# Dense chunks of a two-layer transformer kernel keep their GpSimd form through the MoE routing, and the chunks are shared out anew over the stages

## The chip, the core and the metric

The kernel runs on one core of a Trainium2 chip. A core has a matrix engine (TensorE, in the profile PE, its weight loads PEld), VectorE (DVE), ScalarE (ACT), GpSimd (POOL) and SyncE (SP), which only issues transfers here. Every engine works through its own queue in order, and engines wait for each other through semaphores. The metric is the device time of one execution in microseconds; less is better.

## What is computed

The input is x with 4 sequences of 512 tokens and 256 features, all in float32. Two layers are added to it:

```python
xn = layernorm(x)
x = x + linear_attention(xn) + top32_gene_ffn(xn)          # layer 0
xn = layernorm(x)
x = x + attn_with_dense_ffn(xn) + moe(xn)                  # layer 1
# attn_with_dense_ffn: q,k,v; y = sigmoid(q) * cumsum(exp(k) v) / cumsum(exp(k))
#                      x + (u * silu(g)) @ w_out.T,  u,g = split(y @ w_swiglu.T)
# moe: 16 experts, the best 2 for each token, and one shared expert of twice the width
```

The part that matters here is layer 1. Each token goes through a dense feed-forward (1024 hidden features) and the shared expert (352 hidden features). It also goes through two of 16 experts, for which the tokens are first sorted by expert.

## The kernel before, in words

**Dense chunks.** The dense feed-forward and the shared expert of layer 1 are worked off together by the generator `dense()`. A half is 256 tokens; there are 8 halves, and each has 11 chunks of up to 128 hidden features, 88 chunks in all, numbered here from 0. For one chunk, `up` makes gate and up products in a PSUM bank pair `gu` (matmuls at L583, three such buffers), then tanh at L587 (tile `th`, two buffers), then the hidden tile `hid` (four buffers). `down` (L606), which runs two chunks behind, adds the chunk's contribution to the PSUM accumulator `acc`. After a half's eleventh chunk, L617 adds `acc` to x.

**Two forms of a chunk.** From `gu` and `th` to `hid` there are two ways. In the DVE form (L590, L591) VectorE reads `gu` straight from PSUM in two operations, and `gu` is free when these are done. In the POOL form ScalarE copies `gu` to SBUF (L594, tile `both`), which frees `gu`, and GpSimd does three operations (L595 to L597). The list `calm` says which: as long as it is empty, chunks take the POOL form; L705 fills it.

**Order.** The stages are written as generators and woven together by `together`; `d(n)` gives the next n chunks to a stage. This source order is a priority: when the program is built, the language's scheduler sets the order on each engine, and it moves chunks forward to where it reckons an engine to be free. The chunks are given out so: 40 in the mixing of both layers (L644 to L702), 5 beside the routing (L706), 15 beside the scatters (L708), 6 behind them (L710), and 22 behind the experts.

**Mixing, routing, scatters, experts.** `mix(3, 0, NT)` is the last mixing stage. Its end is on VectorE: scans at L426, reciprocals at L435 and products at L433 and L437, which make `yT`. `route` then counts tokens for each expert: two matmuls on PE (L491, L492) with matrices that GpSimd makes (L472 to L488), a copy of the counts (L494), and a row of small VectorE operations to `slot` (L538), the row of the sorted list to which each token goes. `scatter` writes the tokens there with 32 indirect transfers from GpSimd's queue (L549). These are paced: each also waits for the latest `down` that the source order had reached (`beat`). When all have landed, `fetch` (L741, SyncE's queue) reads the sorted tokens two tiles at a time. The experts run from the transpose at L733 through L770 to L791 and L802. Behind them come the last 22 chunks, beside the gathers of the results (L836).

**Memory.** `const` and `wd` are pools that live to the end; `wk` and `w2` belong to the mixing and are closed at L703, and the pool of the routing takes their place. The constant tile `ones` is read by the scans of the first layer (L274) and of the mixing (L426).

## Time and profile before

| what | value |
|---|---|
| median of 5 runs (lowest, highest) | 589.59 us (588.74 to 589.77) |
| the profiled execution's own time | 589.25 us |
| its span in the profile | 587.5 us |
| mean granted TensorE clock | 0.985 of full speed |
| busy: PE, DVE, ACT, POOL | 540.1, 342.3, 265.8, 235.9 us |
| 88 chunks: up matmuls, L583 | 124.3 + 49.6 us |
| 88 chunks: down matmuls, L606, most of them | 68.5 us |
| POOL form, L595, 40 chunks | 29.7 us, 742 ns each |
| DVE form, L590, 48 chunks | 20.0 us, 418 ns each |
| scatters, L549 | 32 of 966 ns |

PE is busy for 92% of the span, so what is left of the time lies mostly in places where PE stands idle or its clock is halved. The busy share of a span counts matmuls whose ends are modelled. A wait that a view puts down to an engine is put down to the last releaser that the profile knows.

### The profile page before, as it was taken

To read this page: it belongs to the slowest core of one execution; us is meant where nothing else is said; L and a number is where in the kernel's file an instruction comes from. 1 tells how busy PE (TensorE), PEld (TensorE's weight loads), DVE (VectorE), ACT (ScalarE), POOL (GpSimd) and SP (SyncE) were. 2 spreads that over 40 slices of the span, in tenths; PEclk is the share of its full clock that TensorE was granted. 3 is DMA by queue.
4 is the path that set the end of the run, shared out by engine and by line. 5 is a ranking of instruction groups with operands and counts; after the bars stand their busy time and mean duration, and the time that the engine had idled before them with its cause. 6 is when DMAs were issued, how large, how long until landed. Compare 5 with 4: busy or idle time off the path is not lost.

```text
span 587.5 us, 7343 instructions
## 1 busy us (share of the span) xinstructions
PE 540.1 (92%) x2360; PEld 387.7 (66%) x2360; DVE 342.3 (58%) x890; ACT 265.8 (45%) x568; POOL 235.9 (40%) x298
## 2 busy tenths in 40 slices
PE   3958979899999998999899859999999999999997
PEld 1424447655676565766676648887777777788886
DVE  3899998379691948963681786332222222226563
ACT  3667864865447582477348401113333333321111
POOL 1333049476747345573784115770000000007561
PEclk9998979999999999999999979999999999999999
DMA  5993000000000000000029701224333333113541
GB/s 165 388 382 119 1 1 1 1 1 1 1 1 1 0 2 1 2 0 1 0 61 324 206 1 64 103 104 125 90 108 108 108 108 99 55 64 109 142 134 45
DMA packets 38453, 47.38 MB, mean 81 GB/s; under 512 B 4016, under 2 KB 34960, under 8 KB 38160
## 3 DMA queue, kind: packets, MB, share of 16 engines
q1 hardware_dynamic: 35344, 38.53, 20.2%
q0 software_dynamic: 3072, 8.39, 4.7%
q8 instruction: 19, 0.31, 0.2%
q14 instruction: 18, 0.15, 0.1%
HBM read 28.30 MB, written 18.61 MB: 80 GB/s over the span
## 4 chain that ended last, share of the span: by engine, by line
PE 50%; DVE 27%; POOL 7%; ACT 7%; issue 4%; DMA 3%; SPq 0%; POOLq 0%; DVEq 0%; ACTq 0%
PE gu L583 12%; PE pu L770 9%; PE py L791 7%; PE acc L606 6%; PE pm L389 5%; DVE rep L312 5%; DVE top L311 5%; PE pt L733 4%; POOL ys L836 3%; DVE sums L435 3%; DVE sums L426 2%; PE pm L224 2%; PE pm L334 1%; DVE bs L203 1%; DMA wqkv<-in_wqkv_dram 1%
## 5 line engine op out<-in xcount | busy, mean ns | idle before, releaser
L583 PE MATMUL gu<-yT,wugt 128*128 128x256 f32 x512 | 124.3, 381 | 0.0
L583 PEld LDWEIGHTS gu<-yT,wugt 128*128 128x128 f32 x512 | 95.6, 190 | 13.6 <-issue 1.4
L587 ACT ACTIVATE th<-gu 128x256 f32<-128x256 f32 (+1 forms) x88 | 33.7, 383 | 150.8 <-PE gu L583 124.9
L836 POOL DMA_INDIRECT ys<-yrows,slot x32 | 30.3, 948 | 147.1 <-PE acc L606 142.8
L606 PE MATMUL acc<-wot,hid 128*128 128x256 f32 x256 | 68.5, 385 | 8.0 <-DVE hid L591 8.0
L770 PE MATMUL pu<-wex,xgT 128*128 x188 | 63.8, 461 | 0.8 <-ACT xgT L747 0.8
L606 PEld LDWEIGHTS acc<-wot,hid 128*128 128x128 f32 x256 | 47.8, 192 | 15.6 <-DVE hid L591 8.4
L583 PE MATMUL gu<-xn1T,sgu 128*128 128x256 f32 (+1 forms) x192 | 49.6, 394 | 0.1
L779 DVE TENSOR_TENSOR hb<-pu,hb 128x176 f32<-128x176 f32 x47 | 16.0, 341 | 51.0 <-ACT hb L778 51.0
L389 PE MATMUL pm<-w,xn1T 128*128 128x512 f32 (+1 forms) x128 | 44.1, 494 | 0.5 <-ACT xn1T L377 0.5
L791 PE MATMUL py<-wex,hgT 128*128 x188 | 44.5, 379 | 0.0
L595 POOL TENSOR_TENSOR hid<-both 128x256 f32<-128x256 f32 (+1 forms) x40 | 29.7, 742 | 33.5 <-ACT both L594 33.3
L590 DVE SCALAR_TENSOR_TENSOR th<-th,gu 128x256 f32<-128x256 f32 (+1 forms) x48 | 20.0, 418 | 39.2 <-ACT th L587 38.9
L583 PEld LDWEIGHTS gu<-xn1T,sgu 128*128 128x128 f32 (+1 forms) x192 | 35.5, 190 | 9.1 <-issue 2.6
L791 PEld LDWEIGHTS py<-wex,hgT 128*128 128x128 f32 x188 | 35.7, 190 | 8.6 <-issue 0.2
L770 PEld LDWEIGHTS pu<-wex,xgT 128*128 128x128 f32 x188 | 32.0, 190 | 11.0 <-ACT xgT L747 1.0
L549 POOL DMA_INDIRECT xrows<-xn,slot x32 | 30.9, 966 | 20.4 <-DVE th L590 10.9
L389 PEld LDWEIGHTS pm<-w,xn1T 128*128 128x128 f32 x128 | 24.0, 190 | 21.6 <-issue 16.5
L783 DVE COPY hgT<-pt 128x512 f32<-128x512 f32 (+1 forms) x24 | 16.3, 680 | 34.3 <-PE pt L733 34.3
L283 PE MATMUL pm<-wct,xnT 128*128 128x512 f32 x64 | 32.2, 637 | 1.2 <-ACT xnT L242 1.2
L311 DVE MAX8 top<-rep 128x8 f32<-128x512 f32 x48 | 32.6, 680 | 0.3
L312 DVE MATCH_REPLACE8 rep<-top,rep 128x512 f32<-128x512 f32 x48 | 32.3, 673 | 0.0
(170 smaller groups left out, 966.7 us busy)
## 6 DMA issues: line engine op xcount, KB each, us to landing
xrows<-zero SPq DMA_DIRECT2D x1, 6016.0 KB, 22.5
xg<-xrows SPq DMA_DIRECT2D x23, 256.0 KB, 2.8
yrows<-yg SPq DMA_DIRECT2D x23, 256.0 KB, 2.1
wex<-in_w_gate_up_dram SPq DMA_DIRECT2D x8, 704.0 KB, 10.6
xs<-in_x_dram SPq DMA_DIRECT2D x4, 512.0 KB, 7.7
wugt<-in_wug_dram SPq DMA_DIRECT2D x1, 2048.0 KB, 12.5
wex<-in_w_down_dram SPq DMA_DIRECT2D x4, 512.0 KB, 11.6
out_dram<-xs SPq DMA_DIRECT2D x7, 256.0 KB, 2.8
```

The lines of the kernel that those rows point to most:

```text
L283: T.matmul(pl, xnT[:, h, i * P : (i + 1) * P], wct[:, h], start=(h == 0), stop=(h == NH - 1))
L311: V.max(tp[:, 8 * r : 8 * r + 8], src)
L312: V.match_replace(rep, tp[:, 8 * r : 8 * r + 8], src, TAKEN)
L389: T.matmul(o[:, 0:n], xnT[:, h, i * P : (i + 1) * P], w1[:, h, at : at + n], start=(h == 0), stop=(h == NH - 1),)
L549: sc = G.indirect_dma_start(out=xrows, out_offset=bass.IndirectOffsetOnAxis(ap=slot[:, k, i : i + 1], axis=0), in_=xn1[:, i // NT, i % NT] ...
L583: T.matmul(gu[0:m, k], w[:, h, at : at + m], ins[which][:, h], start=(h == 0), stop=(h == NH - 1))
L587: S.activation(th[0:m], gu[0:m, 0], AF.Tanh, scale=0.5)
L595: G.tensor_tensor(hid[0:m], both[0:m, 0], both[0:m, 1], ALU.mult)
L606: mm = T.matmul(acc[:, t], hid[0:m, t * P : (t + 1) * P], dw[0:m, dc], start=(n == 0 and t == 0), stop=(n == NC - 1), skip_group_check=True,)
L770: T.matmul(pg[:, 0 : 2 * NI], xT[:, i, h], wex[:, bass.ds(at[i] + h * 2 * NI, 2 * NI)], start=(h == 0), stop=(h == NH - 1),)
L791: mm = T.matmul(py[:, i * D : (i + 1) * D], hT[:, i, h], wex[:, bass.ds(at[i] + EW - (2 - h) * D, D)], start=(h == 0), stop=(h == 1),)
L836: G.indirect_dma_start(out=ys[:, asked], out_offset=None, in_=yrows, in_offset=bass.IndirectOffsetOnAxis(ap=slot[:, k, n : n + 1], axis=0) ...
```

## The change

```diff
-    ones = const.tile([P, L], F32, name="ones")
-    G.memset(ones, 1.0)
...
+    ones = wk.tile([P, L], F32, name="ones")
+    G.memset(ones, 1.0)
...
-                both = w2.tile([P, 2, HB], F32, name="both")
+                both = wd.tile([P, 2, HB], F32, name="both")
...
-    together((m2, 9), (back(3, 0, NT), 12), d(9))
+    together((m2, 9), (back(3, 0, NT), 12), d(8))
...
-    together((m3, 9), d(5), (load_experts(), 17))
+    together((m3, 9), d(4), (load_experts(), 17))
     mixing.close()
     routing = ctx.enter_context(ExitStack())
-    calm.append(True)
     together((route(), 8), d(5))
     routing.close()
-    together((scatter(), 33), d(15))
-
-    run_all(islice(dd, 6))
+    calm.append(True)
+    together((scatter(), 33), d(18))
+
+    run_all(islice(dd, 5))
```

The five chunks that the source gives to the routing now take the POOL form, since `calm` is filled after the routing. Two chunks fewer are given to the mixing (38 in place of 40), so 43 chunks in all have the POOL form instead of 40. The scatters get 18 chunks in place of 15, and 5 in place of 6 follow them. The sum up to the experts stays 66. For the POOL form to work after the mixing's pools are closed, `both` moves to the pool `wd` (two buffers of 2 KB a partition), and to make room `ones` (2 KB) moves from `const` to `wk`, so that GpSimd fills it a little later. Nothing of the computation changes.

## The prediction

> **What bounds the kernel now.** I read the waits of PE first, because PE is busy for 92% of the span: its largest single wait behind the start is one of 8.0 us.

> ```profile
> PE acc L606 <- DVE hid L591: 8.0, 1, 8.0
> ```

> (engine, line, releaser; total, times, longest, in us.) The timeline shows where it lies: between the end of the last mixing and the routing.

> ```profile
> 334.33 1.89 PE L583 MATMUL gu<-yT,wugt 128*128 128x256 f32 x8
> 338.50 3.36 DVE L435 RECIPROCAL sums<-sums 128x256 f32<-128x256 f32 x2
> 341.77 1.16 DVE L426 TENSOR_TENSOR_SCAN sums<-ones,pm 128x512 f32<-128x512 f32 x1
> 342.85 0.40 DVE L590 SCALAR_TENSOR_TENSOR th<-th,gu 128x256 f32<-128x256 f32 x1
> 343.16 0.69 DVE L437 TENSOR_TENSOR yT<-sums 128x512 f32<-128x512 f32 x1
> 343.76 0.42 DVE L591 TENSOR_TENSOR hid<-gu,th 128x256 f32<-128x256 f32 x1
> 344.24 0.80 PE L606 MATMUL acc<-wot,hid 128*128 128x256 f32 x1 [8.02 <-DVE hid L591]
> ```

> (start, duration.) PE has made the up products of chunk 43 and then needs `hid` of chunk 41. That chunk has the DVE form, and its two operations stand behind the mixing's reciprocals and scan in VectorE's queue. Until they come, all three `gu` buffers are held and PE stands still. The table of stretches adds what follows (length, then busy PE, PEld, DVE, ACT, POOL, clock, DMA share, GB/s):

> ```profile
> 336.00:340.00 4.00, 0.22 (x1) 0.00 (x0) 4.00 (x4) 0.00 (x0) 0.00 (x0) 1.00 0.01 2
> 340.00:344.00 4.00, 0.00 (x0) 0.00 (x0) 4.00 (x6) 0.00 (x0) 0.00 (x1) 0.65 0.00 0
> 344.00:345.00 1.00, 0.76 (x2) 0.67 (x3) 0.82 (x3) 0.38 (x1) 1.00 (x5) 0.50 0.00 0
> 347.00:348.00 1.00, 1.00 (x4) 0.82 (x3) 0.62 (x2) 0.00 (x0) 0.00 (x0) 0.50 0.00 0
> 348.00:349.00 1.00, 1.00 (x6) 0.89 (x5) 0.93 (x3) 0.00 (x0) 0.00 (x0) 0.97 0.00 0
> ```

> The granted clock is halved from about 341.2 to 348.0, so PE also works slowly just when the routing needs it. ACT and POOL are idle here. From the routing on, two chains run to the experts: PE's chunks (2.59 us each: an up row at 361.39, the next at 363.98), and scatter and fetch:

> ```profile
> 347.27 0.42 DVE L494 COPY cnt<-pr 128x256 f32<-128x256 f32 x1 [1.49 <-PE pr L492]
> 356.24 0.17 DVE L538 TENSOR_SCALAR slot<-two 128x32 int32<-128x32 f32 x1
> 396.69 0.96 POOL L549 DMA_INDIRECT xrows<-xn,slot  x1 [0.30 <-issue]
> 399.24 0.88 SPq L741 DMA_DIRECT2D xg<-xrows  x2
> 405.26 0.27 PE L733 MATMUL pt<-ident,xg 128*128 128x128 f32 x1
> ```

> The first fetch is issued at 399.24 and lands 2.7 us later (the transfers of `xg`), at 401.94. PE takes it up at 405.26 without a wait. So today PE's chain ends last, and the scatter chain has only 3.3 us to spare. That number decides this case.

> **The change, part by part.** I read the order of the built program on each engine, before and after. Up to the last mixing's end (ACT's exponentials near 329.5) no engine's order or wait changes, apart from the start. The two chunks taken from the mixing in the source are therefore not taken from it in the program; what differs follows.

> *Three more POOL-form chunks, 40 to 42.* In PE's order, behind the up products of chunk 43, there now stand down 41, up 44, down 42 and up 45, and only then the down that waits for VectorE, now that of chunk 43. Are they fed? ACT copies `both` of chunk 40 after its exponentials (to 330.1), then tanh and copy of 41 (0.38 + 0.58 us, to 331.1), and of 42 once PE has made it (333.66, to 334.7). POOL ends L417 at 330.0 and needs 3 x 0.73 plus gaps, 2.35 us a chunk: `hid` 40 at 332.5, 41 at 334.9, 42 at 337.4. PE wants them at 333.46, 336.1 and 338.7. All are in time, with 0.9 us or more to spare. So PE works on to 334.33 + 3 x 1.73 + 2 x 0.86 = 341.2, and waits about 3.0 us in place of 8.0. VectorE's order behind it is the same, so `hid` (now of 43) still comes at 344.2. Gain for PE: two chunks, 5.2 us. The DVE operations of chunk 40, which go, stood at 326.42 and 326.88 in front of an idle stretch of 2.85 us: worth nothing.

> *The clock.* From PE's rows I listed the stretches of over 2.5 us in which PE runs nothing but transposes or nothing at all. After 221.07 to 224.04 (2.97 us) and 284.33 to 287.01 (2.68) the clock stays at 1.00. After 40.27 to 45.37 (5.10), 73.38 to 80.85 (7.47, with transposes in it) and 336.22 to 344.24 (8.02) it is halved, for 3.4 us once and 6.8 twice. The stretch here becomes 3.0 us, so the nearest row, 2.97, says that the clock stays. The bounds are that the drop stays (nothing gained) or goes. If it goes, L491 and L492, which lie on the way to `cnt`, take 0.43 us each as the full-speed rows of this shape (0.86 for four passes at L606) in place of 0.85 and 0.87, and the half `down` before them shrinks likewise. L491 must still wait for POOL's matrix (L472 to L473, ready at 344.6). I get `cnt` at 346.15 in place of 347.27: 1.1 us earlier. I take this value.

> [...]

> *The routing on VectorE.* From `cnt` to the end of `slot` the trace has 347.27 to 356.41, 9.14 us, with two pairs of chunk operations and L617 inside. After, L617 stands earlier but still inside, and there are two pairs and one more L590: 0.33 us more. `slot` ends at 346.15 + 9.14 + 0.33 = 355.6, against 356.41: 0.8 us earlier; 0.3 us later without the clock's gain.

> *Scatters.* POOL's interval is 1.265 us (395.43, 396.69). The pacing asks for 1.41 us each now (18 chunks of 2.59 for 33 steps), but it starts from earlier beats: the last scatter waits for down 57 in both programs, which was done near 389.9 before (six chunks before 405.42) and is two chunks earlier now. It waits for none. From the end of `slot` to the landing of the first `xg` is 401.94 - 356.41 = 45.5 us as before: landing at 401.1.

> *PE to the experts.* Behind 344.24 PE needs 0.43 each for half a down, L491, L492 and the other half, with the wait for POOL's matrix to 346.3, then 20 chunks of 2.59: 398.1. It therefore waits 3.0 us for `xg`, and the first transpose is at 401.2 against 405.26: **4.1 us earlier**. Of the 7.2 us that PE gains, the scatter chain lets 4.1 through.

> *Costs at nothing.* `ones` is filled after `zero` (0.30 us later); its first reader is at 24.9 us. The expert loads wait for other beats; they are issued to 323.8 and needed at 406. `both` in `wd` keeps two buffers. The fetches behind the first land at 402.7, 404.4 and 405.0 in the trace, 0.8 us earlier after; PE needs the second 2.6 us after the first, so they are in time. The experts and the last 22 chunks keep their order. Bounds for all of these together, from the runs' spread: 0.5 us either way.

> **Sum.** 589.25 - 4.1 = 585.15 for the profiled execution; the median lies 0.34 above that execution, so I forecast **585.5 us** (0.7% faster).

> **Rivals.**
> 1. *The clock takes part of it back* (0.24). If it drops at 341 all the same, `slot` ends at 356.74 and the transpose comes at 402.3: 3.0 us gained, 586.6. Or it drops ahead of the experts: there PE has nothing but transposes from 398.1 to the first L770 at 402.55 (1.35 us behind the first transpose, as 405.26 to 406.61), 4.45 us, which lies between the 2.97 that passed and the 5.10 that did not. Half speed for 3.4 to 6.8 us, less some stalls there, costs 1.5 to 3 us: 587.0 to 588.5. I give the forecast more, since 4.45 us is a drop in some executions at most and the median goes with the majority.
> 2. *PE sets the start of the experts* (0.04): 7.2 us, 582.4. It needs the scatters 3 us faster; at 0.96 + 0.30 us each nothing in the change does that.
> 3. *The chunks don't fill the hole* (0.09): ACT or POOL come late, PE waits for POOL where it waited for DVE, and the time stays at 589.6. Against: the margins above.
> 4. *Slower* (0.09): POOL's nine operations of 0.73 us, new between 330 and 337.4, hold up VectorE's scans and reciprocals, which are the path to `slot`. If each holds VectorE for its whole length, that is 6.6 us: `slot` at 363.3, `xg` at 408.9, 3.6 us later than 405.26: 593.2. It decides from 3.3 us on (`slot` behind 359.7). Against it stands a row pair:

> ```profile
> 227.23 3.33 DVE L435 RECIPROCAL sums<-sums 128x256 f32<-128x256 f32 x2
> 227.61 0.74 POOL L341 TENSOR_TENSOR xw<-xn,nwb 128x256 f32<-128x256 f32 x1
> ```

> With POOL beside it the pair of reciprocals takes 3.33 us, alone 3.36. Only L437 shows a longest of 1.41 us against a median of 0.68: 0.73 us is the most from one meeting, and POOL should be done at 337.4, before 337.9.

> [...]

> **How the numbers follow.** The forecast case has 0.54, between 584.4 and 586.3. The rivals have 0.24, 0.04, 0.09 and 0.09. The range 583.8 to 588.4 takes in the forecast and nearly all of rival 1 (0.77), and reaches a little towards 2 and 3. Faster by over 0.2% (1.2 us, about what a measurement of this kernel can tell): 0.54 + 0.24 + 0.04 = 0.82; same 0.09; slower 0.09.

> **What would show it.** PE's wait for `hid` L591 falls to about 3 us; the clock stays at 1.00 from 341 to 348; L595 runs 43 times; `slot` ends near 355.6; the first L733 is near 401.2, and PE or its weight load waits some 3 us there for the transfer of `xg`; everything behind is the same, 4.1 us earlier. The prediction is wrong if `slot` is later than in the trace of before, if the clock drops, or if PE doesn't wait for `xg`.

## The result, and the profile after

The changed kernel takes a median of 589.29 us (586.73 to 590.12, 24 runs). The kernel before, run beside it, takes 589.49 us (588.11 to 590.64, 44 runs). The ratio is 0.9994, with a 95% interval of 0.9988 to 1.0000: no difference by the bound of 0.2%. The profiled execution took 589.88 us, its span is 588.2 us. L595 runs 43 times.

The waits of PE after the change (engine, line, releaser; total, times, longest):

```profile
PE acc L606 <- DVE hid L591: 2.8, 1, 2.8
...
PE pt L733 <- DMA xg<-xrows: 2.7, 1, 2.7
```

The first part of the prediction came true to within 0.3 us: the wait for `hid` went from 8.0 to 2.8 us (predicted 3.0), and a new wait for the sorted tokens of 2.7 us (predicted 3.0) stands at L733. So PE's hole is filled as meant, and yet the time is the same. The timeline shows how far the gain gets:

```profile
344.82 0.99 PE L606 MATMUL acc<-wot,hid 128*128 128x256 f32 x2 [2.84 <-DVE hid L591]
...
347.55 0.42 DVE L494 COPY cnt<-pr 128x256 f32<-128x256 f32 x1 [1.20 <-PE pr L492]
...
357.14 0.17 DVE L538 TENSOR_SCALAR slot<-two 128x32 int32<-128x32 f32 x1
...
397.60 0.96 POOL L549 DMA_INDIRECT xrows<-xn,slot  x1 [0.30 <-issue]
...
402.97 0.97 PE L733 MATMUL pt<-ident,xg 128*128 128x128 f32 x4 [2.67 <-DMA xg<-xrows]
...
404.67 2.71 PE L770 MATMUL pu<-wex,xgT 128*128 x4 [0.73 <-DMA xg<-xrows]
```

The reader must look at the durations as well as at the starts. The four transposes at L733 take 0.97 us together and the four passes at L770 2.71 us. Before, the first four transposes took 0.60 us and the first four passes stood so:

```profile
406.61 1.45 PE L770 MATMUL pu<-wex,xgT 128*128 x4 [0.75 <-ACT xgT L747]
```

The table of stretches after the change says why (length, then busy PE, PEld, DVE, ACT, POOL, clock, DMA share, GB/s):

```profile
340.00:344.00 4.00, 1.98 (x10) 1.39 (x8) 4.00 (x5) 0.00 (x0) 0.00 (x0) 1.00 0.01 2
344.00:345.00 1.00, 0.18 (x1) 0.19 (x2) 1.00 (x3) 0.15 (x1) 0.45 (x3) 1.00 0.00 0
345.00:346.00 1.00, 1.00 (x3) 0.76 (x3) 0.82 (x4) 0.24 (x1) 1.00 (x3) 0.54 0.00 0
...
400.00:402.00 2.00, 0.30 (x2) 0.00 (x0) 0.74 (x2) 0.00 (x0) 0.00 (x0) 1.00 0.33 92
402.00:404.00 2.00, 0.97 (x4) 0.60 (x4) 0.00 (x0) 0.00 (x0) 0.00 (x0) 0.78 0.95 304
...
406.00:408.00 2.00, 2.00 (x7) 1.38 (x6) 0.23 (x1) 0.32 (x1) 0.00 (x0) 0.50 0.13 45
```

There are two drops of the granted clock. The first comes at 345.08, a quarter of a microsecond after PE has gone back to work, and lasts 3.4 us. Before, it lay at 341.24 to 348.07, so it has moved and become shorter, but it still lies on the two count matmuls ahead of `cnt`. The second is new: 403.11 to 409.94, 6.8 us, at the very start of the experts. There the kernel before had 1.00.

To compare milestones, each trace is shifted so that the start of its last operation at L352 (an addition on VectorE) falls on that of before (300.60). For this kernel that takes off 0.56 us; 0.32 us of it are there at the first matmul (10.06 against 9.74). Milestones below are in this common frame; times of drops and of profile lines are each trace's own. The last column is the 32nd matmul at L791, some 27 us into the experts.

| kernel | `cnt` L494 | `slot` ends | last scatter | first L733 | first L770 | 32nd L791 |
|---|---|---|---|---|---|---|
| before | 347.27 | 356.41 | 396.69 | 405.26 | 406.61 | 429.88 |
| after | 346.99 | 356.75 | 397.04 | 402.41 | 404.11 | 429.88 |

The experts start 2.85 us earlier (405.26 - 402.41), and at the 32nd matmul at L791 nothing is left of it. **The gain is made, and given back within the next 27 us.**

### The profile page after: what moved, and what is told of

Same layout as the page of the kernel before. It is cut to its first block, busy times and chain, and to the rows that moved or that the text cites. A ratio compares the mean times of both kernels' runs of the same rounds, so it can differ in the third digit from the quotient of the medians.

```text
span 588.2 us, 7352 instructions
## 1 busy us (share of the span) xinstructions
PE 543.7 (92%) x2360; PEld 389.6 (66%) x2360; DVE 340.3 (58%) x884; ACT 267.5 (45%) x571; POOL 242.4 (41%) x307
## 4 chain that ended last, share of the span: by engine, by line
PE 46%; DVE 24%; POOL 9%; DMA 8%; ACT 7%; issue 5%; SPq 1%; POOLq 0%; DVEq 0%
PE pu L770 10%; PE gu L583 8%; PE py L791 7%; PE pm L389 5%; DVE rep L312 5%; DVE top L311 4%; PE acc L606 4%; DMA xrows<-xn,slot 4%; PE pt L733 4%; DVE sums L435 3%; POOL ys L836 3%; DVE sums L426 2%; POOL xrows L549 2%; PE pm L283 2%; PE pm L224 2%
## 5 line engine op out<-in xcount | busy, mean ns | idle before, releaser
L583 PE MATMUL gu<-yT,wugt 128*128 128x256 f32 x512 | 124.2, 381 | 0.0
L583 PEld LDWEIGHTS gu<-yT,wugt 128*128 128x128 f32 x512 | 95.6, 190 | 13.6 <-issue 1.2
L606 PE MATMUL acc<-wot,hid 128*128 128x256 f32 x256 | 68.2, 384 | 2.9 <-DVE hid L591 2.8
L770 PE MATMUL pu<-wex,xgT 128*128 x188 | 65.9, 473 | 0.7 <-DMA xg<-xrows 0.7
L606 PEld LDWEIGHTS acc<-wot,hid 128*128 128x128 f32 x256 | 47.6, 191 | 10.4 <-DVE hid L591 3.2
L583 PE MATMUL gu<-xn1T,sgu 128*128 128x256 f32 (+1 forms) x192 | 49.5, 394 | 0.1
L595 POOL TENSOR_TENSOR hid<-both 128x256 f32<-128x256 f32 (+1 forms) x43 | 31.9, 742 | 33.6 <-ACT both L594 33.3
L791 PE MATMUL py<-wex,hgT 128*128 x188 | 44.5, 379 | 0.0
L583 PEld LDWEIGHTS gu<-xn1T,sgu 128*128 128x128 f32 (+1 forms) x192 | 35.4, 189 | 9.2 <-issue 2.6
L791 PEld LDWEIGHTS py<-wex,hgT 128*128 128x128 f32 x188 | 35.7, 190 | 8.6 <-issue 0.2
L770 PEld LDWEIGHTS pu<-wex,xgT 128*128 128x128 f32 x188 | 33.0, 196 | 11.4 <-ACT xgT L747 1.1
L549 POOL DMA_INDIRECT xrows<-xn,slot x32 | 30.9, 967 | 20.7 <-PE gu L583 12.5
L590 DVE SCALAR_TENSOR_TENSOR th<-th,gu 128x256 f32<-128x256 f32 (+1 forms) x45 | 18.7, 417 | 33.6 <-ACT th L587 33.6
L597 POOL TENSOR_TENSOR hid<-hid,th 128x256 f32<-128x256 f32 (+1 forms) x43 | 33.1, 770 | 3.2
L596 POOL TENSOR_TENSOR th<-th,hid 128x256 f32<-128x256 f32 (+1 forms) x43 | 32.4, 752 | 3.3
```

Source lines behind the costliest of these rows:

```text
L549: sc = G.indirect_dma_start(out=xrows, out_offset=bass.IndirectOffsetOnAxis(ap=slot[:, k, i : i + 1], axis=0), in_=xn1[:, i // NT, i % NT] ...
L583: T.matmul(gu[0:m, k], w[:, h, at : at + m], ins[which][:, h], start=(h == 0), stop=(h == NH - 1))
L595: G.tensor_tensor(hid[0:m], both[0:m, 0], both[0:m, 1], ALU.mult)
L596: G.tensor_tensor(th[0:m], th[0:m], hid[0:m], ALU.mult)
L597: G.tensor_tensor(hid[0:m], hid[0:m], th[0:m], ALU.add)
L606: mm = T.matmul(acc[:, t], hid[0:m, t * P : (t + 1) * P], dw[0:m, dc], start=(n == 0 and t == 0), stop=(n == NC - 1), skip_group_check=True,)
```

## The experiments

**The theory** from these profiles: filling the idle stretch works, but (a) the 2.84 us that are left of it still halve the clock ahead of `cnt`, so that the experts start 2.85 us earlier and not 4.1; and (b) the new wait of 2.67 us for `xg` halves the clock again, for 6.8 us at the start of the experts, which costs the 2.85 us. **The rivals:** the 2.85 us go to something else in the experts (fetches, other engines, the memory), whatever the clock does; or the new division of the chunks has a price of its own. Kernels that ran on the same chip are compared with the kernel before on that chip.

### The changed kernel again

No edit; it is the yardstick for the three that follow, on the same chip.

> The changed kernel as it is, beside the others on the same chip. Theory: 588 to 590 where the kernel before has 589.5; in its trace the clock drops behind PE's wait for xg and PE's gain of nearly 3 us at the first transpose is gone some 8 us later. If this chip holds the engines up beside the scatters as in the runs before (four idle stretches that no wait explains, 10 us in all), this control shows by how much.

Measured: 589.40 us against 589.80, ratio 0.9990 (0.9979 to 1.0000). In its profile the first drop begins at 343.76 and still stands from 348 to 349 (0.50), so it lasts over 5.2 us, `slot` ends at 358.04 and the first L733 is at 403.73, 1.5 us earlier than before; the second drop lasts 3.4 us (405.20 to 408.61), and the 32nd L791 is at 430.08, 0.2 us later than before. The two drops vary in length, and the gain is gone in this execution too: the longer first drop took more of it ahead of the experts, the shorter second one less behind (1.7 us).

### Work in place of the wait for the sorted tokens

The gate products of one chunk ahead of the experts are made three times more, into the same place with the same result, about 2.6 us of matmuls that nobody needs:

```diff
+    AGAIN = {65: 3}
...
-            for k, (w, at) in enumerate(((gw, g0), (uw, u0))):
+            pairs_ = ((0, gw, g0), (1, uw, u0))
+            for k, w, at in pairs_[:1] * again + pairs_:
...
-                behind.append((half, n, up(ins, bool(calm), *c)))
+                behind.append((half, n, up(ins, bool(calm), AGAIN.get(half * NC + n, 0), *c)))
```

(`up` gets the argument `again`; lines behind L583 are two further down in this kernel.)

> As e1: the changed kernel with 6 more matmuls in chunk 65, the last before the experts, so that PE isn't idle while it waits for xg. Theory: the clock stays at 1.00 from 400 to 410 and the time is 2.8 us below that of the changed kernel on the same chip. Rival: no difference, or slower by the added matmuls.

Measured: 586.97 us against 589.80, ratio 0.9953 (0.9939 to 0.9967): 2.8 us faster than the kernel before. Against the changed kernel on this chip (589.40) it is 2.4 us, by useless work alone; 2.8 were expected. Its timeline and stretches at the start of the experts:

```profile
404.02 1.44 PE L772 MATMUL pu<-wex,xgT 128*128 x4 [0.74 <-DMA xg<-xrows]
```

```profile
404.00:406.00 2.00, 1.98 (x9) 1.45 (x10) 0.16 (x1) 1.64 (x3) 0.00 (x0) 1.00 0.76 235
406.00:408.00 2.00, 1.98 (x8) 1.10 (x7) 0.53 (x2) 0.83 (x2) 0.00 (x0) 1.00 0.56 139
```

The four passes take 1.44 us instead of 2.71, and the clock stays at 1.00. In the common frame `slot` ends at 356.85 and the first L733 is at 402.45, as in the changed kernel to 0.1 us, while the 32nd L791 is at 427.08, which is 2.80 us earlier. The fetches were not changed, and the transfers' share in these two stretches is higher than in the changed kernel (0.76 and 0.56 against 0.63 and 0.13). So the second drop costs the 2.85 us, and the rival that puts them down to fetches or memory falls.

### A real chunk in place of the wait

```diff
-    run_all(islice(dd, 5))
+    run_all(islice(dd, 6))
```

> As e3: the changed kernel with 6 in place of 5 chunks behind the scatters, 21 in the tail. Theory: 5.4 us below the changed kernel on the same chip (2.8 for the clock, 2.6 for the chunk); rival (the clock costs nothing): 2.6 us below.

Measured: 583.47 us, ratio 0.9898 (0.9880 to 0.9916), 5.9 us below the changed kernel, where 5.4 were expected. The stretch 404 to 406:

```profile
404.00:406.00 2.00, 2.00 (x11) 1.42 (x10) 0.34 (x1) 1.64 (x3) 0.00 (x0) 1.00 0.49 149
```

The clock holds here too, and the 32nd L791 is 2.56 us earlier than before. A chunk that is done there is also missing at the end of the program, which by a chunk's length is worth another 2.59 us (an estimate). The rest of the 6.0 us by which this kernel is below the one before, about 1 us, lies behind the experts and was not followed.

### Both ends filled

The POOL form stays as in the changed kernel, but the mixing gets its 40 chunks back (45 of POOL form in all), the scatters 15, and 8 chunks follow them; the gathers at the end are paced for the two chunks fewer that are left there (two more lines, not shown).

```diff
-    together((m2, 9), (back(3, 0, NT), 12), d(8))
+    together((m2, 9), (back(3, 0, NT), 12), d(9))
...
-    together((m3, 9), d(4), (load_experts(), 17))
+    together((m3, 9), d(5), (load_experts(), 17))
...
-    together((scatter(), 33), d(18))
+    together((scatter(), 33), d(15))
...
-    run_all(islice(dd, 5))
+    run_all(islice(dd, 8))
```

> The changed kernel's forms and memory with the old split, so that 45 chunks have the POOL form and a third chunk stands in the stretch where PE waited, and with 8 chunks behind the scatters (68 before the experts, 20 in the tail, whose gathers and adds are paced a little faster to fit). Theory: PE has no idle stretch over 1 us at 342 nor ahead of the experts, the clock stays up at both, slot comes 1.5 us earlier than in the changed kernel, and the first transpose is near 401.3 where the kernel before has 405.3; with a tail two chunks shorter the time is 9 us below the kernel before: 580. Rival (the tail is then bound by the gathers, 32 at 1.27 us and what follows): 3 to 4 us of that are not won.

Measured: 579.60 us (579.39 to 580.07), ratio 0.9831 (0.9816 to 0.9847): 1.7% faster than both kernels, the fastest version here. Stretches and timeline:

```profile
345.00:346.00 1.00, 1.00 (x7) 0.87 (x6) 0.80 (x3) 0.00 (x0) 1.00 (x2) 1.00 0.00 0
...
402.00:404.00 2.00, 1.92 (x9) 1.45 (x10) 0.08 (x1) 1.63 (x3) 0.00 (x0) 1.00 0.64 161
```

```profile
400.75 0.60 PE L733 MATMUL pt<-ident,xg 128*128 128x128 f32 x4
```

PE has no wait for `hid` and none at the first L733, and the clock is 1.00 in both places. In the common frame `cnt` comes at 345.74 (1.53 us earlier than before), the first L733 at 400.80 (4.46 earlier) and the 32nd L791 at 425.40 (4.48 earlier): what is gained ahead of the experts now arrives behind them. With two chunks less at the end (2 x 2.59) that makes 9.7 us; measured are 10.0 (589.80 x 0.0169).

### The first idle stretch filled alone

The same repeated products, but in chunk 45, ahead of the routing's counts: `AGAIN = {45: 3}`.

> As e8: busy PE in the stretch ahead of the routing. Theory: 1.6 us below the changed kernel's 0.999 of the kernel before (ratio 0.996 to 0.997) if the chip is undisturbed beside the scatters; PE's wait for xg and the clock's drop behind it stay. Rival: no difference to the changed kernel.

Measured: 586.87 us against 589.72, ratio 0.9963 (0.9950 to 0.9976), as the theory had it. Its wait at the first transpose, and the stretches at both ends:

```profile
PE pt L735 <- DMA xg<-xrows: 2.3, 1, 2.3
```

```profile
345.00:346.00 1.00, 1.00 (x6) 0.84 (x5) 0.84 (x3) 0.00 (x0) 0.61 (x3) 1.00 0.00 0
...
402.00:404.00 2.00, 2.00 (x4) 0.90 (x3) 0.00 (x0) 0.71 (x1) 0.00 (x0) 0.50 0.43 144
```

Without the first drop `cnt` is at 345.81 and `slot` ends at 355.11, 1.6 us earlier than in the changed kernel: the size of the term that the prediction took (1.1 us) and a little more. The first L733 is at 400.78. But PE waits 2.3 us there, until 400.11 in the trace's own time, the clock drops for 3.4 us behind that (401.43 to 404.84), and of 4.48 us won at L733, 2.81 are left at the 32nd L791: this drop costs 1.7 us.

### The forms alone, with the old division of the chunks

The changed kernel with 40, 5, 15 and 6 chunks: the first three hunks of the kernel with both ends filled, and `islice(dd, 6)`; the gathers' pacing stays as in the changed kernel.

> As e9: the POOL form with the old split, 45 chunks in the POOL form. Theory: slot 1.6 us earlier than in the changed kernel, over 5 us of wait for xg and the clock halved behind it: ratio about 0.997. Rival (the new split spoils the gain): 0.993 or below.

Measured: 586.36 us, ratio 0.9950 (0.9937 to 0.9962), between what the theory and its rival gave. Its wait and a stretch:

```profile
PE pt L733 <- DMA xg<-xrows: 4.6, 1, 4.6
```

```profile
402.00:404.00 2.00, 1.85 (x3) 1.18 (x4) 0.00 (x0) 1.38 (x2) 0.00 (x0) 0.50 0.70 191
```

With 45 chunks of POOL form the first stretch is filled wholly and the clock stays there; `slot` ends at 354.64 and the first L733 is at 400.43, 4.83 us earlier. PE now waits 4.6 us for `xg`, to 400.33 in the trace's own time. The clock drops at 398.22, while PE still waits, and is back at 405.04. So about 2 of the 6.8 us pass in a wait that would be there anyway, and the drop costs 1.9 us of the 4.83. The drop came as expected; the price in the expectation was too high, since it had no room for the part that falls into the wait.

### A wait shortened by 0.9 us

`AGAIN = {65: 1}`: the gate products made once more.

> As e10: 2 more matmuls only ahead of the experts, a stretch of 3.5 us without matmuls other than transposes. Theory (a window of 3.4 us busy for a fifth or less halves the clock): a drop in about half of the executions, times between 587 and 589. Rival (only a wholly idle window does): as e5, ratio 0.995, no drop.

```profile
PE pt L735 <- DMA xg<-xrows: 2.1, 1, 2.1
```

```profile
404.00:406.00 2.00, 1.49 (x7) 1.05 (x8) 0.00 (x0) 1.72 (x3) 0.00 (x0) 1.00 0.82 254
```

Measured: 586.86 us (585.40 to 588.63), ratio 0.9957 (0.9940 to 0.9973). By the ratio and the profile the rival is nearer: there is no drop, and the 32nd L791 is 2.58 us earlier than before. The expectation had counted the transposes as part of the idle stretch; PE runs nothing for 2.06 us. But the drops above came without 3.4 us of nothing, too: behind waits of 2.3 and 2.7 us, and behind the 2.84 us ahead of `cnt`, the clock fell to 0.50. Nor does the fifth that the theory took as its border hold if transposes count: in the trace of before the clock falls at 78.41, behind 3.41 us of which PE ran for 1.15 (34%), all of it transposes. Two executions took 588.2 and 588.6 us; whether these had a drop, no trace says.

### The division alone, with the old forms

```diff
+    calm.append(True)
     together((route(), 8), d(5))
     routing.close()
-    calm.append(True)
     together((scatter(), 33), d(18))
```

> As e4 and e11: split and memory alone, DVE form. Theory: ratio 1.000, PE waits 8 us for hid and none for xg. Rival: part of the gain at the first transpose, ratio 0.998 or below.

Measured: 589.45 us, ratio 0.9996 (0.9987 to 1.0004). Its wait and its first transposes:

```profile
PE acc L606 <- DVE hid L591: 8.0, 1, 8.0
```

```profile
405.50 0.60 PE L733 MATMUL pt<-ident,xg 128*128 128x128 f32 x4
```

PE waits 8.0 us again and everything stands where it stood before, to 0.1 us at each milestone. The division neither helps nor costs by itself: the forms fill the hole, and the rival of the division's own price falls. Together with the forms it does matter. The old division, with 45 chunks of POOL form, has a ratio of 0.9950 to the kernel before (the run of the forms alone), the changed kernel with 43 has 0.9990 to 0.9994: the old one fills the hole wholly, and the drop ahead of `cnt` is gone.

### Eight runs on two other chips

Six of the kernels above ran on two other chips as well, two of them twice. There the kernel before took about 600 us too, and so did each of these.

> The changed kernel, with the gate products of chunk 65, the last before the experts, made four times in place of once (6 more matmuls, 2.6 us), so that PE has no idle stretch while it waits for the first tokens. Theory (the clock, halved from 403.1 to 409.9 after the wait for xg, eats the gain): the clock stays at 1.00 there, the first transpose is still near 403 in its trace, and the time is 2.8 us below the changed kernel's 589.3: 586.5. Rival (the experts' start is bound by the fetches and the first pairs' chain, the clock is a by-product): the time stays at 589.3 or is above it by the added matmuls.

> The changed kernel, with the gate products of chunk 45 made four times, so that PE is busy from 342.0 to 344.6 where it waited 2.8 us for hid. Theory (the drop at 345 costs the routing 1.1 us): the clock stays at 1.00 there, slot ends and the first transpose comes 1.1 us earlier; but PE is at the experts 1.6 us earlier still, waits longer for xg, and the clock drops there in nearly every execution, so that the time falls by about 1 us only: 588.3. Rival (the routing is bound by VectorE, not by L491 and L492): slot doesn't move, 589.3.

> The changed kernel with 6 chunks in place of 5 behind the scatters, so 67 before the experts and 21 behind. PE fills its wait for xg with a real chunk of 2.6 us. Theory: the clock stays up ahead of the experts (2.8 us) and the tail is a chunk shorter (2.6 us): 583.9. Rival (the clock there costs nothing): only the chunk is won, 586.7. Third: the tail is bound by the gathers, and only the clock is won, 586.5; the profile tells this from the second by the clock and by where the experts begin and end.

> The changed kernel's split of the chunks (38, 5, 18, 5) and its memory, but calm filled ahead of the routing as before, so that the routing's five chunks keep the DVE form. Theory (the POOL form of chunks 40 to 42 is what fills PE's 8 us): PE waits 8 us for hid again, and the time is that of the kernel before, 589.5. Rival (the split does it): PE's wait shrinks without the POOL form, and the first transpose comes earlier than in the kernel before.

> As e2: the changed kernel with 6 more matmuls in chunk 45, so that PE is busy in the stretch ahead of the routing. Theory: no drop of the clock at 344, slot and the first transpose 1.6 us earlier than in the changed kernel; PE is at the experts 1.7 us earlier too, so that its wait for xg and the clock's drop behind it stay: 1.6 us below the changed kernel, about 587.8. Rival (the routing is bound by VectorE alone): no difference.

> One part alone: the POOL form through the routing and both in wd, with the old split (40, 5, 15, 6), so that 45 chunks have the POOL form. Theory: a third chunk fills the stretch ahead of the routing, no drop there, slot 1.6 us earlier than in the changed kernel; PE is at the experts another 2.6 us earlier, waits over 5 us for xg and the clock drops behind that in every execution: 588.0, so that of the 7 us and more that PE has won hardly 2 are left. Rival (the new split is what spoils the gain): clearly faster than the changed kernel, 585 or below.

> The changed kernel with only 2 more matmuls (0.9 us) in chunk 65, so that the stretch without matmuls other than transposes ahead of the experts is 3.5 us in place of 4.4. Theory (a window of 3.4 us that is busy for a fifth or less halves the clock; 18% did, 30% did not): the drop comes in about half of the executions, and the times lie in two groups, near 587 and near 588.5 to 589.5. Rival (only a wholly idle window does): a drop in hardly any, 587.0 as in e5.

> As e4: the new split and the new places in memory alone, the routing's five chunks in the DVE form. Theory: PE waits 8 us for hid as in the kernel before, doesn't wait for xg, and the time is that of the kernel before (589.5 to 589.8). Rival: the split alone gives part of the gain at the first transpose.

| edit | time, us | before there, us | ratio (95%) |
|---|---|---|---|
| products again in chunk 65, three times | 604.57 | 600.01 | 1.0065 (1.0040 to 1.0089) |
| products again in chunk 45 | 600.25 | 600.01 | 0.9992 (0.9968 to 1.0015) |
| one chunk more ahead of the experts | 602.20 | 600.01 | 1.0024 (1.0005 to 1.0044) |
| division alone | 600.83 | 600.01 | 1.0008 (0.9989 to 1.0027) |
| products again in chunk 45, again | 600.11 | 600.74 | 1.0012 (0.9994 to 1.0030) |
| forms alone | 601.00 | 600.74 | 0.9999 (0.9976 to 1.0022) |
| products again in chunk 65, once | 603.00 | 600.74 | 1.0045 (1.0020 to 1.0069) |
| division alone, again | 598.93 | 600.74 | 0.9981 (0.9959 to 1.0003) |

The division alone was expected to give nothing and gave nothing. None of the other six runs gave the gain expected, and three came out slower by their intervals (1.0065, 1.0045, 1.0024). The waits of the second row's kernel between 357 and 405 us show what was different, beside the scatters:

```profile
DVE th L592 <- issue: 20.5, 3, 9.8
ACT th L589 <- remote: 19.8, 2, 10.3
```

(`issue` and `remote`: released by no engine and no transfer that the profile knows.) ScalarE and VectorE stand still for up to 10 us at a time, and PE waits behind them. The traces of before, of the changed kernel and of its repeat have no such wait beside the scatters: there VectorE's longest is 1.7 us and ScalarE's 2.5 us. In the common frame the first L733 comes at 412.5 to 420.3 in these eight traces, against 400.4 to 405.3 in the others. So these ratios don't tell what the edits do where nothing stands still, and what the same edits gave above was not seen on these chips. Ahead of the scatters the traces agree with those of the other chips: with the products in chunk 45 there is no drop near 344, with those in chunk 65 three times PE waits 2.8 us for `hid`, and with the division alone 8.0 us.

## Why the prediction was wrong

It said 585.5 us, 583.8 to 588.4; the time is 589.29, outside the range and without a measurable change.

**Right.** The reading of the bound, the filling and the new wait: PE's wait for `hid` fell to 2.8 us (predicted 3.0), and PE then waited for the sorted tokens, 2.7 us (predicted 3.0). Rivals 3 and 4 did not happen: the chunks came in time, and VectorE's way to `slot` took only 0.3 us longer than in the sum (below). That POOL's operations hold up VectorE for their whole length, the 6.6 us of rival 4, no run shows: in the common frame PE's wait for `hid` ends at 344.26, before at 344.24. Rival 2 did not happen either: PE waited for the sorted tokens, so the scatter chain set the start of the experts.

**The step that failed is the paragraph on the clock**: "the nearest row, 2.97, says that the clock stays". It failed twice, at both ends.

- *Ahead of `cnt`.* The drop stayed. The row that was leaned on, 221.07 to 224.04 in the trace of before, is not an idle stretch of 2.97 us. It ends so:

```profile
223.57 0.63 PE L224 MATMUL pm<-ident,vs 128*128 128x128 f32 x4 [1.63 <-DVE dn L339]
```

PE ran nothing for 1.63 us (in brackets, the idle time before), and then transposes. The list had counted transposes as idle. The stretch after the change has no transposes in it: 2.84 us of nothing. It was compared with the wrong row. By the prediction's own second sum, "without the clock's gain", `slot` ends at 356.74; measured is 356.75, and the first L733 at 402.41 (the prediction's 402.3). That `slot` fits to 0.01 us is luck: `cnt` came 0.28 us earlier than before (346.99 against 347.27), and from there to the end of `slot` it took 9.76 us in place of the 9.47 in the sum. What this end cost is 4.1 - 2.85 = 1.25 us.

- *Ahead of the experts.* The prediction had this mechanism in rival 1 and a price of 1.5 to 3 us, measured 2.85 (and 1.7 where it lasted 3.4 us). It went wrong in two ways. The two drops stood there as alternatives, "if it drops at 341 all the same ... or it drops ahead of the experts", and the range held no case with both; the first case's 586.6 and the measured price of the second make 586.6 + 2.85 = 589.45; the median is 589.29. And the chance was argued down: "a drop in some executions at most". Both profiles of the changed kernel have both drops, and its median, close to the sum with both, suggests that most executions do.

The prediction priced the new wait for `xg` as harmless in itself, since PE was ahead anyway. What it missed is that this wait of 2.67 us in front of the experts was paid again behind it, by 2.85 us.

**The 1.1 us of the sum** rested on the row of 2.97 us; in the changed kernel they were not there, and with the first stretch filled `slot` came 1.6 us earlier than in it. The row from 73.38 to 80.85 is no idle stretch of 7.47 us either: PE's longest idle stretch in it is 3.38 us, 73.38 to 76.75, and transposes follow it up to the drop at 78.41. Shorter idle stretches had a drop behind them as well: 2.3, 2.67 and 2.84 us (next but one section).

**What stays open.** How often an execution of the changed kernel has each drop, and how long, is not known from two profiles. What stood in them is listed in the next but one section. The lowest execution of the changed kernel, 586.73 us, may be one without the second drop; that was not seen.

## What to carry to other kernels

Filling an idle stretch of the busiest engine moves it forward until the next thing that is late, and the new wait in front of that is part of the change's price: here 2.7 us of waiting for sorted tokens halved the clock of the matmuls behind it and took the whole gain. When asking whether the clock holds, look at how long PE runs at all in the stretch ahead (here the drops in two traces came behind 3.41 us in which it ran for at most 1.15, transposes included), and price all drops together, not one instead of the other. What was worth 1.7% was to fill both ends with real chunks and to move two chunks forward from the end of the program.

## What was not expected of the hardware

The stretches around the experts' start, in the changed kernel:

```profile
399.70:403.11 3.41, 0.74 (x5) 0.36 (x4) 0.85 (x2) 0.16 (x1) 0.00 (x0) 1.00 0.51 162
403.11:406.53 3.42, 2.69 (x7) 1.60 (x7) 0.00 (x0) 1.87 (x2) 0.00 (x0) 0.50 0.68 221
406.53:409.94 3.41, 3.41 (x10) 2.22 (x9) 0.34 (x1) 0.90 (x2) 0.00 (x0) 0.50 0.15 29
```

- **How long a drop lasted.** These seven drops make twelve such stretches at 0.50. Full clock came back after seven, in which PE ran for 2.81, 2.96 and five times 3.41 us or more; after the other five, with 0.41, 2.62, 2.69, 2.75 and 2.88 us, the clock stayed at 0.50. In the lines above it was 2.69 us and then 3.41.
- **The length of a wait was a rough guide only.** From 40 us on PE runs nothing for over 1.2 us 13 times in these two traces: six stretches of 1.36 to 1.66 us had no drop behind them, and the seven of 2.67 to 8.02 us had one or lay in one. Behind the waits of 2.8 us in front of `acc` the clock is 0.50 to 0.54 from 345 to 346 in five profiles (the changed kernel, its repeat, the products in chunk 65 three times and once, and the real chunk). With the products in chunk 45 a wait of 2.3 us had a drop behind it, with those made once in chunk 65 one of 2.06 us had none.
- **Whether transposes count as work was not settled.** With them the most ahead of these drops is 1.15 us and the least elsewhere 1.78; without them it is 0.60 us (ahead of 403.11) and 1.03.
- **The drop fell on the wait or behind it.** In the changed kernel it begins at 345.08, after PE has worked again for 0.26 us, and falls on work; with the forms alone it begins at 398.22, 2.1 us before PE's wait ends.
- **Engines that stood still.** On two chips ScalarE and VectorE stood still for up to 11.6 us at a time beside the indirect scatters, in all eight profiles, and the kernel before took 600 instead of 589.5 us. The cause is open.
